# Graph attention with residual layer norm: three more output products put off to the end, unpaired norms after the last block, and the output bias of other late tiles added by VectorE

## The chip, the cores and the metric

The kernel runs on one core of one Trainium2 chip. The metric is device time in microseconds (us), the median of three runs. Engines are called PE (TensorE, matrix products), DVE (VectorE), ACT (ScalarE), POOL (GpSimd) and SP (SyncE, which here only issues DMAs). Line numbers such as L799 are those of the kernel before, as its profile shows them.

## The reference

One layer: multi-head attention over a graph, an output projection, a residual sum and a layer norm without scale or shift. x has 16 batches of 1024 rows of 512 numbers; there are 8 heads of 64. adj is a 1024 x 1024 matrix of zeros and ones, drawn with probabilities that fall with the row and column index, so most rows have few ones.

```python
q = (x @ Wq + bq).reshape(b, n, H, HD)
k = (x @ Wk + bk).reshape(b, n, H, HD)
v = (x @ Wv + bv).reshape(b, n, H, HD)
scores = jnp.einsum('bqhd,bkhd->bhqk', q, k) / jnp.sqrt(jnp.float32(HD))
scores = scores + (1.0 - adj)[None, None, :, :] * -1000000000.0
attn = jax.nn.softmax(scores, axis=-1)
out = jnp.einsum('bhqk,bkhd->bqhd', attn, v).reshape(b, n, d)
x = _layernorm(x + out @ Wo + bo)      # (y - mean) / sqrt(var + 1e-5)
```

## The kernel before

**Tiles.** The kernel sorts the rows of adj by their number of ones and works on 8 tiles of 128 rows per batch, rows of like degree together. A tile is named by batch and number, (b, t), and counted as 8 b + t. Batches from the third on are handled in pairs for the rows with the fewest neighbours; tile "mean" rows, tile 8 and tile 9 (`LONE_TILE`, `MORE_TILE`) collect such rows.

**Fronts.** For each batch PE transposes x and forms q, k and v (L757, L799 as `pq`, L956); the results go to DRAM. The list `fronts` holds these products as units with a cost, for all batches in order.

**Blocks.** Attention is done sparsely: one block is one neighbour of each of 128 rows. POOL gathers the neighbours' k and v by an indirect DMA (L1269), DVE multiplies and reduces (L1290, L1294), ACT takes the exponential (L1305) and weighs v (L1318) or DVE does (L1322), and DVE adds the block to the tile's sum (L1334). For tiles 6 and 7 a few deeper blocks are added on PE (`sum`, L1343 and L1344). When a tile closes, `normalise` divides by the denominator (L1355 to L1364), PE transposes the result (`poT`, L1378) and ACT copies it to `oT` (L1382).

**Output.** `finish(b, t)` then issues the output product of the tile, `po`, four units on PE (L799, each two records in the trace), and `complete` adds residual and bias on DVE with the row sum (L1108, L1109), squares on ACT (`spread`, L1116), scales the variance on DVE (L1119), takes the power -1/2 on POOL (L1122, or L1152 for two tiles at once), forms the shift on DVE (L1125), normalises on ACT (L1130) and stores rows by an indirect DMA from POOL (L1134). The output bias goes in one of three ways: as long as there are fronts (`plain`) DVE adds it in L1109; after that a small bf16 product on PE adds it within the output product (L1087); after the last block DVE adds it to the residual (L1076).

**Put-off tiles.** Tiles in `SPILL` don't get their output product in their own batch. Their `oT` is stored to DRAM by SP (L1384) and loaded again once the fronts are used up (`reload`, L1064), one every second step, into the buffers e, w and g in turn. Tiles in `STORED` have their residual rows saved in sorted order, and SP loads them from there (L1035); other residuals are gathered by POOL (L1038).

**Order.** All instructions are written out by hand in a loop over steps `n`, one per block (`tc.manual_schedule()`); each engine's queue has the order in which the loop issues its instructions. `later(k, fn)` puts a piece k steps on, `later_last` behind the other work of that step. In each step PE units are issued for as long as `credit` lasts, which grows by a share per step. In batches 1 to 12 that share is the PE work which the batch has to get done divided by its steps; `kept`, in that sum, counts the output products of tiles that aren't put off. From batch 13 on the share is set so that the fronts end 12 steps before the last batch, and after that it is 3.4 per step, where a unit of an output product counts 0.86. No product is begun in the last two steps before `total`, the step after the last block. After `total` the loop goes on until all products, stores and the guard (a test of number ranges that writes `flag`) are through.

**Pairs.** Once the fronts are over, norms are done for two tiles at a time: `half` keeps the first until the second comes, one power on POOL serves both. Tiles completed more than 3 steps after `total`, and shorter tiles, are done singly, with several steps between the stages.

Of the kernel before, what the change touches and what calls it, by code (L numbers as in the profile page):

```python
# [41 lines left out]

LAZY = 2

SPILL = (*(8 * b + t for b in range(4, 12) for t in (3, 6)), 102, 103, 106, 107)
STORED = {*SPILL, *(i for i in range(10, 102) if i % 8 in (2, 5, 7)), *(i for i in range(102, 128) if i % 8 > 1)}
LATE = 12

# [26 lines left out]
P = 128  # L75
# [103 lines left out]
def kernel(  # L179
# [75 lines left out]
    with ExitStack() as main:  # L255
# [85 lines left out]
        def tiles_of(b):  # L341
            return [t for t in range(NT) if t or b < PAIRED_FROM or merged(b)]

        def number(b, t):
            return b * NT + t if t < NT else -1
# [3 lines left out]
        x_rows = x.rearrange("b n d -> (b n) d")  # L349
        spill = {i: dram.tile([P, D], F32, name=f"spill_{i}") for i in SPILL}  # L350
        residual = {i: dram.tile([P, D], F32, name=f"residual_{i}") for i in sorted(STORED)}
# [94 lines left out]
        now, plan, rest, urgent, known, waiting, combined = [0], {}, {}, [], [], [], []  # L446

        def later(k, fn):
            plan.setdefault(now[0] + k, []).append(fn)

        def later_last(k, fn):
            rest.setdefault(now[0] + k, []).append(fn)
# [340 lines left out]
        def product(name, lhs, w, out):  # L793

            def unit(c):
                if c == 0:
                    PS[name] = fill_psum(name)
                p = PS[name]
                nc.tensor.matmul(p, lhs(c), w[:, c, :], start=(c == 0), stop=(c == NPAIR - 1))  # L799
                if c == NPAIR - 1:  # L800
                    del PS[name]
                    later(1, lambda: out(p))

            return [(PRODUCT, lambda c=c: unit(c), None) for c in range(NPAIR)]
# [210 lines left out]
        def rows_of(b, t):  # L1015

            if t == LONE_TILE or t == 0 and merged(b):
                n, col, base = (2 * SPARED, NT + 2, b - 1) if t else (P, NT + 1, b - 1)
            elif t == MORE_TILE:
                n, col, base = (LONE - SPARED) * (B - PAIRED_FROM), NT + 3, 0  # L1020
            else:
                n, col, base = P, NT if t == ONE_KEY and b >= PAIRED_FROM else t, b
            return n, asked_row[0:n, col:col + 1], base * N * D
# [30 lines left out]
        def keep_mean(b, p):  # L1054

            m = work.tile([1, D], F32, tag="q", name=f"out_mean_{b}", bufs=2)
            nc.scalar.copy(m, p[0:1, :])
            nc.sync.dma_start(mean_rows[b:b + 1, :], m)
            if merged(b):
                later(2, lambda: lone_tiles.append(b))  # L1060
# [7 lines left out]
        def finish(b, t):  # L1068


            mean_row = t == ONE_KEY and b >= PAIRED_FROM
            plain = bool(fronts) or mean_row
            biased = not plain and now[0] < total

            if now[0] >= total and not plain:
                nc.vector.tensor_tensor(Y[b, t], Y[b, t], bo_bc, op=OP.add)  # L1076

            def out(p):
                OT.pop((b, t))
                if mean_row:  # L1080
                    keep_mean(b, p)
                complete(b, t, p, plain)

            units = product(f"po_{b}_{t}", lambda c: OT[b, t][:, ts(c, P)], W["o"], out)
            if biased:
                def bias():
                    nc.tensor.matmul(  # L1087
                        PS[f"po_{b}_{t}"], three.to_broadcast([P, P]), bo_3, start=False, stop=False
                    )

                units.insert(2, (BIAS, bias, None))
            return units

        def complete(b, t, p, plain):
            n, rows, offset = rows_of(b, t)
            y, p = Y[b, t][0:n, :], p[0:n, :]
            single = fronts or now[0] > total + 3 or n < P
            if single:
                st = small.tile([P, 5], F32, name="stats", bufs=6)[0:n, :]
            else:  # L1100

                second = bool(half)
                if not second:
                    half.append([small.tile([P, 2, 5], F32, name="stats_2", bufs=5)])
                st2 = half[0][0]
                st = st2[:, int(second), :]
            if plain:
                nc.vector.tensor_tensor(y, p, y, op=OP.add)  # L1108
            nc.vector.scalar_tensor_tensor(  # L1109
                y, bo_bc[0:n, :] if plain else p, 1.0, y, op0=OP.mult, op1=OP.add, accum_out=st[:, 0:1]  # L1110
            )

            def spread():

                sq = work.tile([P, D], F32, tag="ysq", name=f"ysq_{b}_{t}", bufs=1)
                nc.scalar.activation(sq[0:n, :], y, AF.Square, bias=st[:, 0:1], scale=-float(D), accum_out=st[:, 2:3])  # L1116

            def variance():
                nc.vector.tensor_scalar(st[:, 2:3], st[:, 2:3], 1.0 / D ** 3, EPS, op0=OP.mult, op1=OP.add)  # L1119

            def power():
                nc.gpsimd.tensor_tensor(st[:, 3:4], st[:, 2:3], neg_half[0:n, :], op=OP.pow)  # L1122

            def shift():
                nc.vector.scalar_tensor_tensor(  # L1125
                    st[:, 4:5], st[:, 0:1], -1.0 / D, st[:, 3:4], op0=OP.mult, op1=OP.mult
                )

            def norm_out():
                nc.scalar.activation(y, y, AF.Identity, bias=st[:, 4:5], scale=st[:, 3:4])  # L1130
                later(2, store)

            def store():
                nc.gpsimd.indirect_dma_start(  # L1134
                    out=out_rows[b, t], out_offset=bass.IndirectOffsetOnAxis(ap=rows, axis=0),
                    in_=y, in_offset=None, element_offset=offset,
                )
                del Y[b, t]

            later_last(1, spread)  # L1140
            if single:
                late = 1 if fronts else 0
                later(2 + late, variance)
                later(3 + late, power)
                later(4 + 2 * late, shift)
                later_last(5 + 2 * late, norm_out)
            elif second:
                later(3, variance)
                mate_shift, mate_norm_out = half.pop()[1]

                def powers():
                    nc.gpsimd.tensor_tensor(  # L1152
                        st2[:, :, 3:4], st2[:, :, 2:3], neg_half[:, :, None].to_broadcast([P, 2, 1]), op=OP.pow
                    )

                def shifts():
                    mate_shift()
                    shift()

                later(4, powers)  # L1160
                later(6, shifts)
                later_last(6, mate_norm_out)
                later_last(7, norm_out)
            else:
                later(3, variance)
                mine = half[0]
                mine.append((shift, norm_out))

                def alone():
                    if half and half[0] is mine:  # L1170
                        half.pop()
                        power()
                        later(2, shift)
                        later_last(3, norm_out)

                later(6, alone)
# [197 lines left out]
        def turn(b, t, o):  # L1374
            def transpose():
# [4 lines left out]
                def out():  # L1380
                    OT[b, t] = work.tile([P, D], F32, tag="oT", name=f"oT_{b}_{t}", bufs=LAZY + 2)
                    nc.scalar.copy(OT[b, t], p)  # L1382
                    if number(b, t) in SPILL:
                        later(1, lambda: nc.sync.dma_start(spill[b * NT + t], OT.pop((b, t))))  # L1384
# [74 lines left out]
        done, coming, spilled, gathered, fronts, guarded = [], [], [], [0], [], []  # L1459

        total = len(blocks)

        def kept_y():
            return sum(t == "mean" or number(b, t) not in SPILL for b, t in Y)

# [25 lines left out]
        with tc.manual_schedule():  # L1491
# [9 lines left out]
            def needed(b, part):  # L1501
                b += int(part)
                if b >= B:
                    return fronts_time
                return fronts_by[b - 1] + (part - int(part)) * (fronts_by[b] - fronts_by[b - 1])
# [6 lines left out]
            n = -LEAD_IN  # L1512
            while n < total or plan or rest or urgent or done or finishing or spilled or lone_tiles or not guarded:
# [6 lines left out]
                elif n in start:  # L1520

                    b = start.index(n)
                    left = sum(u[0] for u in fronts)
                    ahead = EARLY + FIRST * (1 - max(0, b - 1) / LATE)
                    goal = fronts_time - needed(b + 2, ahead / NBT)
                    kept = sum(number(b, t) not in SPILL for t in tiles_of(b))
                    share = (max(0.0, left - goal) + kept * NPAIR * PRODUCT + NS * SUM) / (start[b + 1] - start[b])
# [105 lines left out]
```

## Time and profile before

| what | value |
|---|---|
| median of three runs | 1852.05 us (1851.02 to 1852.08) |
| profiled execution, its own time | 1859.34 us |
| its span, first to last instruction | 1857.6 us |
| PE busy (matmul) | 1807.5 us, 97% |
| DVE busy | 1686.4 us, 91% |
| ACT busy | 1565.1 us, 84% |
| POOL busy | 1247.5 us, 67% |
| mean granted clock of PE | 0.993 |
| output products `po` (L799), mean of one record | 600 ns (they overlap; eight of them follow each other in 3.43 us) |
| bias products (L1087) | 32 |

Busy time adds up what an engine's instructions took, and an idle engine may wait for data or for a buffer. The chain of waits follows the last instruction back through what released it each time. A timeline line gives the start, the length, the engine, the line, the operation and its tiles, and in brackets the idle time before it and what ended it.

### The profile page before, as it was taken

How to read it: one execution, taken by the hardware profiler on the slowest of the kernel's cores; microseconds unless marked ns; L12 is line 12 of the kernel's file. 1: busy time of each engine (PE TensorE's matmuls, PEld its weight loads, DVE VectorE, ACT ScalarE, POOL GpSimd, SP SyncE). 2: the span in 40 equal slices, each digit the busy share in tenths (PEclk: the TensorE clock that was granted, in tenths of full speed). 3: DMA queues.
4: the chain of work that ended last, by engine and by line, in shares of the span. 5: the costliest groups of instructions: out<-in, count | busy, mean ns of one | idle time of the engine just before them, and what ended most of it. 6: DMA issues, size and time to landing. Idle time of an engine off the chain costs nothing.

```text
span 1857.6 us, 25324 instructions
## 1 busy us (share of the span) xinstructions
PE 1807.5 (97%) x5150; PEld 878.6 (47%) x5150; DVE 1686.4 (91%) x3462; ACT 1565.1 (84%) x6184; POOL 1247.5 (67%) x1154
## 2 busy tenths in 40 slices
PE   7999999999999999999999999999999999999995
PEld 3444454544444444454444445454444444444442
DVE  6889889999989999999999999999999999997885
ACT  3637869989888898999789898989899999987885
POOL 1367866777666686667757676677767777665874
PEclk9999999999999999999999999999999999999998
DMA  7357797988888998999989998998989999888983
GB/s 285 111 187 244 245 324 250 335 305 315 301 299 295 312 323 303 330 312 310 316 312 310 331 321 299 342 319 314 346 285 331 318 352 318 311 313 317 361 305 120
DMA packets 195431, 553.82 MB, mean 298 GB/s; under 512 B 33162, under 2 KB 33182, under 8 KB 195266
## 3 DMA queue, kind: packets, MB, share of 16 engines
q0 software_dynamic: 113600, 373.64, 59.7%
q1 hardware_dynamic: 78590, 172.65, 24.9%
q10 hardware_dynamic: 3076, 5.82, 0.9%
q14 instruction: 122, 1.00, 0.2%
q8 instruction: 43, 0.70, 0.2%
HBM read 419.52 MB, written 153.51 MB: 308 GB/s over the span
## 4 chain that ended last, share of the span: by engine, by line
PE 69%; DVE 11%; ACT 8%; DMA 4%; issue 3%; POOL 1%; SPq 0%; POOLq 0%; DVEq 0%; ACTq 0%
PE po L799 17%; PE pq L799 14%; PE pp L956 12%; PE x L956 8%; PE z L956 8%; ACT pv L1318 5%; DVE qk L1290 2%; PE poT L1378 2%; PE pxT L757 2%; DMA kvg<-kv_pair,place_row 2%; DVE s L1294 2%; PE sum L1344 2%; PE sum L1343 2%; ACT sq_k L809 1%; DVE pv L1334 1%
## 5 line engine op out<-in xcount | busy, mean ns | idle before, releaser
L1318 ACT ACTIVATE pv<-kvg,pv 128x64 f32<-128x64 f32 x3600 | 907.3, 341 | 0.0
L1269 POOL DMA_INDIRECT kvg<-kv_pair,place_row x462 | 540.1, 1169 | 283.6 <-ACT pv L1318 89.5
L799 PE MATMUL po<-wo,oT 128*128 128x512 f32 x816 | 376.8, 600 | 0.4 <-ACT oT L1382 0.4
L799 PE MATMUL pq<-wq,xT 128*128 128x512 f32 x792 | 368.7, 597 | 1.9 <-DVE q L830 1.9
L1294 DVE TENSOR_REDUCE s<-qk 128x8 f32<-128x512 f32 x530 | 361.0, 681 | 6.7
L1290 DVE TENSOR_TENSOR qk<-qt,kvg 128x512 f32<-128x512 f32 x434 | 297.1, 685 | 3.1 <-DMA kvg<-kv_pair,place_row 2.9
L799 PEld LDWEIGHTS po<-wo,oT 128*128 128x128 f32 x816 | 155.3, 193 | 177.1 <-issue 167.9
L956 PE MATMUL x<-b,xT 128*128 128x512 f32 x504 | 237.1, 593 | 0.3 <-ACT e L969 0.2
L956 PE MATMUL pp<-t,s 128*128 128x512 f32 x504 | 237.0, 593 | 0.0
L1334 DVE TENSOR_TENSOR pv<-pv,pv 128x520 f32<-128x520 f32 x329 | 228.4, 694 | 3.8 <-ACT pv L1318 3.6
L799 PEld LDWEIGHTS pq<-wq,xT 128*128 128x128 f32 x792 | 148.4, 192 | 165.4 <-issue 152.6
L1010 POOL DMA_INDIRECT x<-in_x_dram,asked_row x120 | 132.3, 1103 | 75.0 <-PE pxT L757 22.1
L1134 POOL DMA_INDIRECT out_dram<-y,asked_row x129 | 146.9, 1139 | 40.4 <-issue 18.4
L1305 ACT ACTIVATE pv<-s,absent 128x8 f32<-128x8 f32 x434 | 126.9, 294 | 46.4 <-DVE s L1294 43.1
L809 ACT ACTIVATE sq_k<-kv 128x128 bf16<-128x128 f32 x512 | 150.8, 301 | 8.0 <-DVE kv L979 5.0
L956 PEld LDWEIGHTS pp<-t,s 128*128 128x128 f32 x504 | 94.3, 190 | 107.6 <-issue 98.4
L956 PEld LDWEIGHTS x<-b,xT 128*128 128x128 f32 x504 | 94.1, 190 | 106.2 <-issue 98.4
L1223 POOL DMA_INDIRECT qg<-q_rows,query_row x96 | 108.4, 1129 | 26.9 <-issue 24.5
L956 PE MATMUL z<-b,s 128*128 128x512 f32 x252 | 119.0, 595 | 3.7 <-DVE kv L984 3.7
L956 PE MATMUL z<-t,s 128*128 128x512 f32 x252 | 118.6, 593 | 0.0
L956 PE MATMUL pp<-t,xT 128*128 128x512 f32 x252 | 118.5, 593 | 0.0
L1130 ACT ACTIVATE y<-y,stats 128x512 f32<-128x512 f32 (+1 forms) x129 | 103.8, 807 | 17.2 <-DVE stats L1125 16.8
(276 smaller groups left out, 2710.4 us busy)
## 6 DMA issues: line engine op xcount, KB each, us to landing
kv_pair<-kv SPq DMA_DIRECT2D x98, 512.0 KB
q_rows<-q SPq DMA_DIRECT2D x106, 256.0 KB
qt<-q_rows SPq DMA_DIRECT2D x98, 256.0 KB
residual<-x SPq DMA_DIRECT2D x71, 256.0 KB
y<-residual SPq DMA_DIRECT2D x71, 256.0 KB
kv_rows<-kv SPq DMA_DIRECT2D x15, 512.0 KB
kvg<-kv_pair,place_row POOLq DMA_INDIRECT x462, 6.8
kv_pair<-kv SPq DMA_DIRECT2D x28, 256.0 KB
```

The lines of the kernel that those rows point to most:

```text
L799: nc.tensor.matmul(p, lhs(c), w[:, c, :], start=(c == 0), stop=(c == NPAIR - 1))
L809: nc.scalar.activation(sq, s[:, ts(h, P)], AF.Square, scale=scale, accum_out=sums[:, h:h + 1])
L956: nc.tensor.matmul(R[bank], l[:, ts(c, P)], right[:, c, :], start=(first and c == 0), stop=(c == 1), skip_group_check=True,)
L1010: nc.gpsimd.indirect_dma_start(out=y, out_offset=None, in_=x_rows, in_offset=bass.IndirectOffsetOnAxis(ap=asked_row[:, t:t + 1], axis=0), ...
L1134: nc.gpsimd.indirect_dma_start(out=out_rows[b, t], out_offset=bass.IndirectOffsetOnAxis(ap=rows, axis=0), in_=y, in_offset=None, element_o ...
L1223: nc.gpsimd.indirect_dma_start(out=q, out_offset=None, in_=q_rows[b % ROWS], in_offset=bass.IndirectOffsetOnAxis(ap=rows, axis=0))
L1269: nc.gpsimd.indirect_dma_start(out=KG[n], out_offset=None, in_=rows, in_offset=bass.IndirectOffsetOnAxis(ap=(place_row if b else key_row)[ ...
L1290: nc.vector.tensor_tensor(QK[n], q, KG[n][:, 0:D], op=OP.mult)
L1294: nc.vector.tensor_reduce(S[n], QK.pop(n).rearrange("p (h d) -> p h d", d=HD), axis=AX.X, op=OP.add)
L1305: nc.scalar.activation(PV[n][:, D:], S.pop(n), AF.Exp, bias=bias)
L1318: nc.scalar.activation(pv[:, ts(h, HD)], v[:, ds(D + h * HD, HD)], AF.Copy, scale=pv[:, D + h:D + h + 1])
L1334: nc.vector.tensor_tensor(PV[b, t], PV[b, t], pv, op=OP.add)
```

## The change

Three tiles join `SPILL`: 45, 69 and 93, that is tile 5 of batches 5, 8 and 11. After the fronts and before `total` only put-off tiles and tile 9 still get the bias as a product on PE; all others get it on DVE, added to the residual when the product begins. If a product ends in the last three steps before `total`, its `complete` is moved to `total`. Tiles completed from `total - 1` on are done singly, with one step from stage to stage, and their square in the step of the sum itself.

```diff
-SPILL = (*(8 * b + t for b in range(4, 12) for t in (3, 6)), 102, 103, 106, 107)
+SPILL = (*(8 * b + t for b in range(4, 12) for t in (3, 6)), 45, 69, 93, 102, 103, 106, 107)
...
-            biased = not plain and now[0] < total
-
-            if now[0] >= total and not plain:
+            biased = not plain and now[0] < total and number(b, t) in (*SPILL, -1)
+
+            if not plain and not biased:
                 nc.vector.tensor_tensor(Y[b, t], Y[b, t], bo_bc, op=OP.add)
 
             def out(p):
                 OT.pop((b, t))
                 if mean_row:
                     keep_mean(b, p)
-                complete(b, t, p, plain)
+                if not fronts and total - 4 < now[0] < total:
+                    later(total - now[0], lambda: complete(b, t, p, plain))
+                else:
+                    complete(b, t, p, plain)
...
-            single = fronts or now[0] > total + 3 or n < P
+            ending = not fronts and now[0] >= total - 1
+            single = fronts or ending or n < P
...
-            later_last(1, spread)
-            if single:
+            later_last(0 if ending else 1, spread)
+            if ending:
+                for step in (variance, power, shift):
+                    later(1, step)
+                later_last(1, norm_out)
+            elif single:
                 late = 1 if fronts else 0
                 later(2 + late, variance)
                 later(3 + late, power)
```

## The prediction

> **What bounds the kernel now.** I read the page first (PE 97%, DVE 91%, ACT 84% of a 1857.6 us span), then the busy times batch by batch, cut where the last reduction of a batch (L1372) stands. Shown are batches 5, 8, 10, 11 and 13; 5, 8 and 11 are those that lose a product.
>
> ```profile
> 702.18:804.59 102.41, 101.52 (x293) 49.69 (x293) 99.08 (x195) 93.36 (x388) 68.72 (x63) 1.00 0.92 321
> 1012.18:1112.54 100.36, 99.96 (x290) 49.17 (x289) 97.09 (x191) 90.62 (x368) 70.98 (x65) 1.00 0.93 320
> 1214.48:1313.24 98.76, 98.70 (x287) 48.58 (x286) 96.39 (x191) 92.23 (x371) 73.96 (x65) 1.00 0.92 327
> 1313.24:1419.84 106.60, 106.37 (x309) 52.13 (x308) 99.66 (x195) 96.14 (x397) 70.41 (x64) 1.00 0.88 311
> 1518.36:1614.15 95.79, 90.75 (x263) 44.32 (x262) 93.01 (x179) 89.56 (x377) 63.29 (x57) 0.98 0.92 323
> ```
>
> Columns: stretch, its length, busy us of PE, PE's weight loads, DVE, ACT, POOL, granted clock, DMA share, GB/s. TensorE lacks 0.2 to 0.9 us per batch, so these batches are as long as its work; VectorE stands just behind, up to 97.6% (batch 10), and in batch 13 (last line), where PE idles 5 us, DVE at 97.1% is what is left as a bound.
>
> Next the chain of waits, in order of time, for the end:
>
> ```profile
> 1785.81 0.22 PE po L1087
> 1786.03 3.43 PE po L799 x8
> ...
> 1828.96 1.19 PE sum L1343 x2
> 1830.16 0.88 PE sum L1344 x2
> 1831.04 3.42 PE po L799 x4
> 1834.45 0.42 PE po L1087
> 1834.88 1.83 PE po L799 x4
> 1836.77 0.58 issue
> 1837.43 0.62 DVE pv L1334
> ```
>
> One output product is eight records, 3.43 us; its bias product adds 0.22. Up to 1815.5 the chain is TensorE's products, then VectorE's, then the slow product of the last but one tile (5.7 us instead of 3.65). Last, the timeline of the tail:
>
> ```profile
> 1832.22 2.00 ACT L1318 ACTIVATE pv<-kvg,pv 128x64 f32<-128x64 f32 x8
> 1836.73 0.69 DVE L1109 SCALAR_TENSOR_TENSOR y<-po,y 128x512 f32<-128x512 f32 x1 [4.24 <-PE po L799]
> 1837.35 0.69 DVE L1334 TENSOR_TENSOR pv<-pv,pv 128x520 f32<-128x520 f32 x1
> 1848.67 0.58 POOL L1122 TENSOR_TENSOR stats<-stats,neg_half 128x1 f32<-128x1 f32 x1 [4.53 <-DVE stats L1119]
> 1849.45 1.04 POOL L1134 DMA_INDIRECT out_dram<-y,asked_row  x1 [0.20 <-issue]
> 1850.79 0.96 POOL L1134 DMA_INDIRECT out_dram<-y,asked_row  x1 [0.30 <-issue]
> ```
>
> The last attention sum (L1334) could start at 1834.2, when ACT's pv ends; it stands behind a y sum that waits 4.24 us for PE. After the last y sum: square, power on POOL, normalise, store; the store of 1850.79 is 6.8 us before the end of the span.
>
> **What the Trainium skill says.** "TensorE: Matmul & The Clock Gate" (Architectural detail) calls ACT and DVE strict FIFOs; the 4.24 us above agree. The same page (Part 1) halves the clock after about one idle window of 3.4 us; the trace shows clock 0.50 from 1830 to 1834 and from 1842 to 1844, after 2.78 and 3.04 us waits with little work around them. "Perfetto Trace Analysis" (Identifying the Most-Contended Engine) warns that matmul busy time is not distance to roofline; I use it only as queue time, since products follow each other every 3.43 us.
>
> **The change, part by part.**
>
> *Three products put off (tiles 45, 69, 93, batches 5, 8, 11).* Each batch loses 3.43 us of PE, and on DVE the two sums of L1108 and L1109 and two small steps: 0.61 + 0.69 + 0.15 + 0.15 = 1.6 us. ACT loses a square and a normalisation (0.9 + 0.8), POOL a power and a store. Added is one spill store on SP's queue (256 KB, 0.32 us to issue); a residual load and an output store of the same size go, so DMA moves 256 KB less of some 32 MB. These tiles are stored as residuals already. Is the 3.43 us got? PE alone says 3 x 3.43 = 10.3. If DVE can't go beyond the 97.6% of batch 10, batch 5 needs (99.08 - 1.6) / 0.976 = 99.9 us, which gains 2.5, batch 8 likewise 97.8, 2.5; batch 11 is still PE's, 3.4. I take 8.4. From below: DVE's own 1.6 each, 4.8; from above 10.3.
>
> *Fewer bias products.* The built order has 22 instead of 32. Up to the transpose of tile 7 of batch 15 as many products stand as before, with ten bias products fewer: 10 x 0.22 = 2.2 us of PE, on the chain up to 1815.5. Between 1720 and 1735 PE already waited 2.2 us for a spill load while DMA was full, so what the first three (po 3, 4, 5 of batch 14) save is likely to wait there: I take 1.5, ends 0 and 2.2. Instead DVE adds L1076, 0.61 us each, ten times before 1815.5. DVE was busy 133 of the 165 us from 1650 on, so these lie beside PE's products. The add stands earlier in the queue than the sum that needed the residual before, and waits for the load: for tile 4 of batch 15 SP issued it at 1787.4, landing takes 5.5 us in the median (2.7 to 7.8), and the add comes at about 1790.9, so 2 us are lost, with the next block's products behind it; DVE's waits for PE of 0.46, 0.58, 1.02, 1.44 and 1.14 us from 1795 to 1815 take that up. SP is not late: the load of po 7's residual waited to 1814.4, then come the last three spill loads, each behind the product that frees its buffer (1815.5, 1819.2, 1822.8); the first is needed at 1826.
>
> *The tail.* I follow the new queues in the times of before (all shifted alike by the two parts above). PE has a put-off product between the transpose of tile 7 and sum 6, then po 7, po 2, the transpose of 6, po 3, po 6. It fills the idle stretches, so the clock matters less; nothing below waits for it, even at half clock. DVE: the y sums of the two products that end near the last block are put behind the last attention sum, so that starts at 1834.2 instead of 1837.35 and o is ready at 1836.5: 3.1 us won. Then DVE does two reductions (0.24), two y sums and one add (1.85), two shifts (0.2): 1838.85. Now each tile has its own variance, power and shift: variance to power 0.24, power to shift 0.62, as at 1848.43, 1848.67, 1849.29, so 0.86 a rung and 0.15 for the shift. Two rungs: 1840.87. The y sum of po 2 (0.61), an add (0.61), the guard's five small steps (0.8): 1842.9, third power 1843.2 to 1843.8.
>
> In POOL's new order three powers stand before three stores, then power, three stores, power, store. A store takes 1.04 and 0.3 to the next. Stores from 1844.0 to 1847.65, fourth power to 1848.3 (its variance was ready at 1845.7: 2 us of queue), three stores to 1852.2, fifth power to 1852.85, shift 1852.9, normalise 1853.15 to 1853.95, store at 1854.2 (0.27 after an ACT end, as at 1831.88). Before: 1850.79. The tail costs 3.4 us, although its products themselves fit. Ends: +1 (powers that pass the stores sooner, because stores issue faster) and +5.5 (0.83 us powers, as at 1842.08, and a late third rung).
>
> *Sum.* -8.4 - 1.5 + 3.4 = -6.5 us. The profiled execution took 1859.34 (span 1857.6 and 1.74 around it), so 1852.8; it is 0.39% above the median of 1852.05, and the same share gives 1845.6.
>
> **Rivals.**
>
> *All of it gained.* PE is the only bound (10.3 + 2.2) and the tail comes out even: 1852.05 - 12.5 = 1839.5. For it: PE's missing 0.2 to 0.9 us per batch. Against: DVE at 96 to 98%, POOL's order.
>
> *The batches don't shorten beyond VectorE's share.* 4.8 gained, the bias saving lost to DMA, tail +3.4: 1850.6. For it: batch 13, and DMA at 0.92. Against: batches 4 to 11, with two tiles put off each, took 102.5 us on average, batches 2 and 3, with none, 105.3 and 112.8.
>
> *Slower: the adds wait for their residuals.* Ten adds stand before 1815.5. DVE's 32 us of idle there, less 6.1 for the adds and 2.2 that PE shortens, leave 24: from a mean wait of 2.4 us each on, DVE is the bound of the end. At 3.6 us the 12 us beyond come on top: about 1857.5. For it: the 2 us at tile 4. Against: most of SP's residual loads issue over 8 us ahead of use.
>
> **How the numbers follow.** Forecast 0.52, all gained 0.18, VectorE's share 0.20, adds late 0.10. What this measurement can't tell from no change is 0.2%, 3.7 us: 1848.35 to 1855.75. Faster: 0.48 of the forecast's 0.52 (its own range is 1841 to 1849.5), 0.18, and 0.05 of the third: 0.71. Same: 0.04 + 0.15 + 0.01 = 0.20. Slower: 0.09. Range 1838.5 to 1852: below it is the lower third of the second case, above it the late adds and the worst of the third.
>
> **What would show it.** Batches 5, 8 and 11 shorter by 2 to 3.4 us, the others as before; DVE at 98% there. 22 records of L1087's successor (L1090). L1076 fourteen times; a wait for a residual load before it at tile 4. The last pv sum right after ACT's pv, no 4.24 us wait. On POOL three stores between the third and fourth power and between the fourth and fifth, and the last store some 3 us later, counted from ACT's last pv. It is wrong if the batches keep their length, if PE waits for spill loads in the last 40 us, or if the last power isn't held up by stores.

## The result, and the profile after

The changed kernel takes 1850.74 us in the median of 12 runs (1847.92 to 1854.60), the kernel before, run beside it, 1854.72 us (1851.02 to 1859.03). The ratio is 0.9983, 95% interval 0.9975 to 0.9991: 0.17% faster, about 3.2 us (1.7 to 4.6 by the interval; the two medians lie 4.0 apart), where 0.35% was forecast. The forecast's 1845.6 us started from 1852.05, the median of three runs; the twelve runs beside the changed kernel put the kernel before at 1854.72. The profiled execution took 1851.61 us (span 1849.8), 7.7 us below the profiled one of before. That pair overstates the gain: the profiled execution of before was one of its longest. Batches 6 and 7 took 207.6 us in it, against 205.4 and 204.4 us in two other kernels that issue the same instructions in the same order there.

The page of the changed kernel, its span and the busy time of each engine:

```profile
span 1849.8 us, 25305 instructions
PE 1800.1 (97%) x5127; PEld 874.5 (47%) x5140; DVE 1691.9 (91%) x3472; ACT 1565.2 (85%) x6184; POOL 1249.1 (68%) x1154
```

The busy times of the changed kernel batch by batch, cut at the last reduction of a batch as before (batches 5, 8, 10, 11 and 13; the columns are those of the prediction: stretch, length, busy us of PE, weight loads, DVE, ACT, POOL, granted clock, DMA share, GB/s):

```profile
701.46:801.41 99.95, 99.57 (x286) 48.27 (x286) 97.73 (x190) 91.94 (x387) 69.18 (x62) 1.00 0.94 330
1005.91:1106.89 100.98, 98.03 (x281) 48.12 (x280) 95.96 (x187) 88.95 (x363) 68.24 (x65) 0.98 0.94 328
...
1209.24:1308.52 99.28, 99.24 (x288) 48.69 (x288) 96.38 (x191) 92.34 (x371) 75.59 (x66) 1.00 0.91 325
1308.52:1411.63 103.11, 102.31 (x300) 50.44 (x300) 98.20 (x191) 94.21 (x393) 67.28 (x62) 1.00 0.90 317
1509.57:1603.96 94.39, 89.69 (x263) 44.14 (x263) 92.89 (x179) 88.56 (x375) 62.88 (x57) 1.00 0.93 328
```

Batch 5 went from 102.41 to 99.95 us and batch 11 from 106.60 to 103.11. Batch 8, which lost a product as well, went from 100.36 to 100.98. It is the line to stop at: PE lacks 2.95 us of the stretch where it lacked 0.40 before, and its clock is 0.98.

The timeline of the tail, DVE and POOL around the last attention sum (start, length, engine, line, operation and tiles, idle time before it and what ended it):

```profile
1823.35 0.70 DVE L1342 TENSOR_TENSOR pv<-pv,pv 128x520 f32<-128x520 f32 x1 [1.75 <-ACT pv L1326]
...
1834.25 0.15 DVE L1123 TENSOR_SCALAR stats<-stats 128x1 f32<-128x1 f32 x1 [0.49 <-ACT ysq L1120]
...
1839.25 0.15 DVE L1123 TENSOR_SCALAR stats<-stats 128x1 f32<-128x1 f32 x1 [0.88 <-ACT ysq L1120]
...
1832.59 1.04 POOL L1138 DMA_INDIRECT out_dram<-y,asked_row  x1 [0.18 <-ACT y L1134]
1833.93 0.96 POOL L1138 DMA_INDIRECT out_dram<-y,asked_row  x1 [0.30 <-issue]
1835.20 0.96 POOL L1138 DMA_INDIRECT out_dram<-y,asked_row  x1 [0.30 <-issue]
1836.19 0.57 POOL L1126 TENSOR_TENSOR stats<-stats,neg_half 128x1 f32<-128x1 f32 x1
1836.95 1.53 POOL L1138 DMA_INDIRECT out_dram<-y,asked_row  x1 [0.19 <-issue]
...
1841.04 0.57 POOL L1126 TENSOR_TENSOR stats<-stats,neg_half 128x1 f32<-128x1 f32 x1
1842.99 1.04 POOL L1138 DMA_INDIRECT out_dram<-y,asked_row  x1 [1.38 <-ACT y L1134]
```

The last attention sum (L1342, which was L1334) now waits only for ACT's pv, which ends at 1823.31. The fourth and fifth powers (L1126) stand behind three stores each: their variances (L1123) were done at 1834.40 and 1839.40, they start at 1836.19 and 1841.04, 1.8 and 1.6 us later. From the end of ACT's last pv to the last store it is 19.7 us, before 16.6.

The chain of waits of the changed kernel (start, length, what held the end up) runs through the same places, from ACT's pv to the last sum and at the end through a store into the fifth power:

```profile
1821.41 1.92 ACT pv L1326 x8
...
1823.35 0.71 DVE pv L1342
...
1840.05 0.96 POOL out_dram L1138
...
1841.04 0.57 POOL stats L1126
```

### The profile page after: what moved, and what is told of

Same layout as the page of the kernel before. It is cut to its first block, busy times and chain, and to the rows that moved or that the text cites. A ratio compares the mean times of both kernels' runs of the same rounds, so it can differ in the third digit from the quotient of the medians.

```text
span 1849.8 us, 25305 instructions
## 1 busy us (share of the span) xinstructions
PE 1800.1 (97%) x5127; PEld 874.5 (47%) x5140; DVE 1691.9 (91%) x3472; ACT 1565.2 (85%) x6184; POOL 1249.1 (68%) x1154
## 4 chain that ended last, share of the span: by engine, by line
PE 72%; DVE 11%; DMA 5%; ACT 4%; issue 3%; POOL 1%; SPq 0%; POOLq 0%; DVEq 0%; ACTq 0%
PE po L799 17%; PE pq L799 15%; PE pp L956 13%; PE z L956 9%; PE x L956 9%; ACT pv L1326 2%; PE pxT L757 2%; DVE qk L1298 2%; PE poT L1386 2%; DVE s L1302 2%; PE sum L1352 2%; PE sum L1351 2%; DMA kvg<-kv_pair,place_row 2%; DVE pv L1342 1%; DMA oTs<-spill 1%
## 5 line engine op out<-in xcount | busy, mean ns | idle before, releaser
L1277 POOL DMA_INDIRECT kvg<-kv_pair,place_row x462 | 532.2, 1152 | 289.0 <-ACT pv L1326 89.8
L799 PE MATMUL po<-wo,oT 128*128 128x512 f32 x792 | 359.2, 593 | 0.2 <-ACT oT L1390 0.2
L1342 DVE TENSOR_TENSOR pv<-pv,pv 128x520 f32<-128x520 f32 x329 | 228.3, 694 | 4.4 <-ACT pv L1326 4.2
L799 PEld LDWEIGHTS po<-wo,oT 128*128 128x128 f32 x792 | 148.6, 190 | 169.5 <-issue 160.6
L1010 POOL DMA_INDIRECT x<-in_x_dram,asked_row x120 | 136.2, 1135 | 65.8 <-issue 21.2
```

The lines of the kernel that those rows point to most:

```text
L1010: nc.gpsimd.indirect_dma_start(out=y, out_offset=None, in_=x_rows, in_offset=bass.IndirectOffsetOnAxis(ap=asked_row[:, t:t + 1], axis=0), ...
L1277: nc.gpsimd.indirect_dma_start(out=KG[n], out_offset=None, in_=rows, in_offset=bass.IndirectOffsetOnAxis(ap=(place_row if b else key_row)[ ...
L1342: nc.vector.tensor_tensor(PV[b, t], PV[b, t], pv, op=OP.add)
```

## The experiments

Ratios are against the kernel before on the same chip. The first four runs fell on a chip whose times are those of above. The others fell on chips where every kernel takes 0.9 to 1.7% longer, most of it in batch 0 (286 to 297 us instead of 277), and where runs of one kernel differ by 10 us and more. There the lengths of batches in the traces tell more than totals, though they scatter too.

*The three products taken out for good.* All three are stored and never fetched again, so their rows of the output are not written:

```
 SPILL = (*(8 * b + t for b in range(4, 12) for t in (3, 6)), 45, 69, 93, 102, 103, 106, 107)
+NEVER = 45, 69, 93
...
-                        spilled.append((b, t))
+                        if number(b, t) not in NEVER:
+                            spilled.append((b, t))
```

> The kernel before, with the attention outputs of tile 5 of batches 5, 8 and 11 stored to DRAM and never fetched again: their output product, layer norm and store of rows are left out for good, so those 384 rows are not written. It measures what the three products cost inside their batches, with nothing given back at the end. My sum says 8.4 us less than before (2.8 a tile; if TensorE's share alone decided, 10.3). The rival that only VectorE's share comes back says 4.8 us less (1.6 a tile). The theory that the rest of the batch takes up the gap (another engine's work becomes the bound there) says under 3 us. If it is 8 or more, the front term of my sum was right and the bias term or the end is what failed.

Measured: 1848.31 us, ratio 0.9963 (0.9947 to 0.9979): 6.9 us less, interval 3.9 to 9.8. The size of the sum is possible, 4.8 is too.

*Only the list of put-off products* (the SPILL line alone).

> The kernel before with only the list of put-off products made longer by three; the bias of the last tiles stays on TensorE and the end keeps its paired norms. The three products move to the last batches, where TensorE has more to do. My sum says that nothing is won by moving work alone unless the last two batches have room for it: the front gives -8.4 us and the end takes three products (10.3 us of TensorE) less the gaps they fill there. In after, batches 14 and 15 were 3.7 us shorter with all parts together. I expect -2 to -5 us against before; the theory that the products find no gap at the end says 0 to +2.

Measured: 1851.36 us, ratio 0.9982 (0.9973 to 0.9991), 3.3 us less: as expected, and as much as the whole change.

*Only the bias.*

```
-            biased = not plain and now[0] < total
+            biased = not plain and now[0] < total and number(b, t) in (*SPILL, -1)
...
-            if now[0] >= total and not plain:
+            if not plain and not biased:
```

> The kernel before with only the bias of the last tiles that were not put off moved from TensorE to VectorE's sum with the residual. My sum says -1.5 us (bounds 0 and -2.2). The rival theory, that TensorE then only reaches its wait for a fetched attention output sooner and loses the time there, says -0.5 to 0. That the sums wait for residuals and hold up VectorE says above 0.

Measured: 1852.42 us, ratio 0.9987 (0.9979 to 0.9995), 2.4 us less (0.9 to 3.9). Alone it brings what I gave it, or more.

*Only the end* (completions put off, norms unpaired; 20 tiles put off as before).

> The kernel before with only the end changed: the last completions are put off until the attention is done, and the norms there are unpaired. Removing the wait at the last attention sum should give 3.1 us there, and the stores in GpSimd's queue between the powers should take some of it back: from ACT's last pv to the end of the span 23.4 us before, 26.5 us in after. Theory: the span from ACT's last pv grows by 2 to 3.5 us, the batch before it shrinks by about 3, so the whole is -1 to +1 us. If the tail change is a pure loss, +2 to +3.5 us.

Measured: 1854.34 us, ratio 0.9999 (0.9991 to 1.0008): nothing, as expected of the total. The way there was not the expected one. The stretch behind ACT's last pv, expected to grow by 2 to 3.5 us, grew by 0.3 (23.69 us, before 23.38).

These four already show where the lack is. Kernels that issue the same instructions in the same order in a batch need nearly the same time for it (the chance of it is seen within each group of three). Lengths in us, from six traces of the same speed:

| batch | before | bias_only | tail_only | after | drop3 | spill_only | with three less |
|---|---|---|---|---|---|---|---|
| 5 | 102.41 | 102.41 | 102.60 | 99.95 | 100.03 | 99.95 | -2.5 |
| 8 | 100.36 | 100.42 | 100.37 | 100.98 | 100.99 | 100.76 | +0.5 |
| 9 | 101.94 | 101.89 | 101.93 | 102.35 | 102.35 | 102.34 | +0.4 |
| 11 | 106.60 | 106.25 | 106.65 | 103.11 | 103.11 | 103.75 | -3.2 |
| 12, 13 | 194.31 | 193.52 | 193.99 | 192.33 | 192.32 | 193.26 | -1.3 |

(12 and 13 are the sum of two; the last column is the mean of the last three kernels less that of the first three.) From the start of batch 5 to the end of 13 it is 908.8 us in the mean of bias_only and tail_only and 902.7 in the mean of the three with the products gone: 6.1 us, where the sum had 8.4. (The trace of the kernel before, 912.0 us, is left out of that mean for its long batches 6 and 7.) Batch 8 gives nothing. Its timeline in the changed kernel, PE first and then DVE:

```profile
1061.42 1.88 PE L956 MATMUL z<-t,s 128*128 128x512 f32 x4
1063.14 1.88 PE L956 MATMUL pp<-t,xT 128*128 128x512 f32 x4
1067.97 3.67 PE L956 MATMUL z<-b,s 128*128 128x512 f32 x4 [2.95 <-DVE kv L984]
...
1065.76 0.42 DVE L783 TENSOR_TENSOR s<-xT 128x256 f32<-128x256 f32 x1 [0.29 <-ACT xT L761]
...
1067.23 0.68 DVE L984 TENSOR_TENSOR kv<-z,g 128x512 f32<-128x512 f32 x1
```

and in the kernel before:

```profile
1067.72 1.88 PE L956 MATMUL z<-t,s 128*128 128x512 f32 x4
...
1071.16 0.60 PE L1378 MATMUL poT<-ident,o 128*128 128x128 f32 x4
1071.59 1.88 PE L956 MATMUL z<-b,s 128*128 128x512 f32 x4
...
1069.64 0.69 DVE L984 TENSOR_TENSOR kv<-z,g 128x512 f32<-128x512 f32 x1 [0.94 <-PE z L956]
```

The two z products of a pair add into one PSUM tile, and VectorE's L984 must read it between them. Before, the plan put the first z product two blocks ahead of the second; L984 (waiting 0.94 us for it) ran as soon as it was done, and the second z found it read. With a product less the plan puts the first z into the block just ahead of the second, L984 into VectorE's next block, behind a score reduction and four sums of 256 columns, and PE stands 2.95 us for it. The product behind the wait runs at half clock (3.67 us for four records instead of 1.88). So PE loses about 4.7 us (2.95 and the 1.79 that the product took longer) where it had been spared 3.43.

On the other chips, in the runs below, the same order repeats less well. Batch 5 took 102.2 us instead of 100.0 in after_again and spill_tail_b, about half of that from work that had moved there out of a shorter batch 4. In spill_tail_b batch 8 took 104.23 us, with longer waits (4.15 us at L984) whose cause I don't know.

*Two products instead of three, and another batch instead of batch 8* (in the changed kernel `45, 93` and `45, 77, 93` in place of `45, 69, 93`).

> The changed kernel with two products put off instead of three: tile 5 of batch 8 is left where it was. In all three traces with that product gone, batch 8 took 0.5 us more than in the three with it (100.91 against 100.38), because TensorE waits 2.95 us for L984's successor once and then runs one product at half clock. Theory that the product of batch 8 brings nothing: batch 8 back at 100.4, batch 9 at 101.9 instead of 102.35, the end shorter by part of a product, 0 to 1 us for the rest, so the whole is 0 to 2.5 us below the changed kernel. Rival: the loss in batch 8 is made good later (in batches 9 to 13, which were 1.4 us shorter together), so it is 1 to 2 us above the changed kernel. My first sum, 2.5 us for this product, says 2.5 us above it.

> The changed kernel with tile 5 of batch 9 put off in place of tile 5 of batch 8. In batch 9 TensorE is busy 101.9 of 101.9 us and VectorE 96.7, so by the shares of my first sum it should lose all 3.4 us, with batch 8 back at 100.4: together 3.5 to 4 us below the changed kernel, batch 9 at 98.5. Rival: what a batch gives back is set by where the new plan puts the neighbours of the missing product and not by the shares, so batch 9 may lose anything from 0 to 3.4 us: -0.5 to -4 us. If the whole is above the changed kernel, both are wrong.

Measured: after_two 1879.55 us, ratio 0.9972 (0.9950 to 0.9994); after_77 1875.67 us, ratio 0.9935 (0.9919 to 0.9952), without the changed kernel beside them. In the traces batch 8 did not come back at 100.4 but took 106.48 and 106.42 us (with all three put off, spill_bias and spill_tail took 99.87 and 100.93 us on the same chip), then batch 9 101.14 and 99.62. Batches 8 to 10 of after_two, by busy times:

```profile
1026.47:1132.95 106.48, 104.40 (x298) 50.38 (x296) 97.16 (x192) 94.33 (x378) 72.40 (x68) 1.00 0.91 315
1132.95:1234.09 101.14, 98.96 (x290) 48.82 (x292) 96.61 (x190) 91.60 (x377) 65.57 (x61) 1.00 0.89 309
1234.09:1336.14 102.05, 99.28 (x286) 48.04 (x285) 96.39 (x190) 92.87 (x371) 72.08 (x65) 1.00 0.90 316
```

PE has as many products as before there (874 records; before 877) and lacks 7.0 us instead of 0.5: a product missing in batch 5 and none in batch 8 makes the plan of batch 8 worse than either of the other lists does. Both my theories on these two fell, and they share their ground: I priced a batch by its shares, or took over the old batch 8, while each list gives a new order. For after_77 the total (11 us less than before, only 6 runs) and its trace (batches 5 to 13 in 910.1 us, the changed kernel 902.5, 908.4 and 903.5 in three traces) don't agree; I leave it open.

*The bias and the end in company*: spill_tail is the changed kernel with the bias on TensorE, spill_bias the one with the old end.

> The changed kernel with the bias of the last tiles back on TensorE (32 bias products instead of 22, no sums of the bias with the residual before the end). Alone, moving the bias brought 2.4 us (interval 0.9 to 3.9). If the saving adds up, this is 1.5 to 2.4 us above the changed kernel. If in company it is lost to the wait for the fetched attention output near 1720 (0.7 us alone, 1.9 us and four records at half clock in the changed kernel), it is within 0.5 us of the changed kernel.

> The changed kernel with the end as before: completions not put off, norms in pairs. Its stores then don't stand between as many powers, but the last attention sum waits again for two products. By my sum the changed end wins 3.1 us at the last attention sum and loses it again behind it, so this is within 1 us of the changed kernel, with the stretch from ACT's last pv to the end longer by about 1 us or shorter by as much. If the changed end is worth its 3 us, it is 2 to 3 us above; if it is a loss, 1 to 3 us below.

Measured: 0.9971 (0.9954 to 0.9987) and 0.9954 (0.9939 to 0.9969), without the changed kernel beside them, so only their traces answer. From ACT's last pv to the end of the span spill_bias takes 26.85 us, the changed kernel 26.49: the new end is worth nothing there, with three more tiles too. With the bias on TensorE it costs 1.1 us there (spill_only, with the old end, 25.39; spill_tail_c 26.48).

*The order of one pair.* The changed kernel, with the first z product of the pair that is prepared in batch 8 issued before the transposes instead of behind them:

```
-            units += xt
-            units += unit("z", s(1), T1, True, out_v1, None)
+            z = unit("z", s(1), T1, True, out_v1, None)
+            units += z + xt if (b, j) == (10, 0) else xt + z
```

> The changed kernel once more, for a second trace and as the measure for the other three runs on this chip. From its first runs: 0.17% below the kernel before (interval 0.09 to 0.25). Batch 8 again with a wait of 2.95 us of TensorE for VectorE's L984, since that comes from the order of the instructions and not from this one execution.

> The changed kernel with one pair's order changed (tiles 0 and 1 of batch 10, which are prepared in batch 8): the first z product stands before the transposes of the next tiles instead of behind them, so VectorE's sum that empties it comes one block earlier and the second z product finds it done. The same instructions, 28 of TensorE's rows moved. Theory: the wait of 2.95 us and the half clock behind it go, batch 8 takes about 98.3 us (VectorE's 95.96 us at its 97.6%), the whole is 2.5 to 3 us below the changed kernel, and the product put off in batch 8 is then worth what my first sum gave it. Rival: TensorE only meets VectorE a few products later, batch 8 and 9 keep 203.3 us together, no change.

> The changed kernel with the bias of the last tiles back on TensorE, again, now beside the changed kernel on the same chip. If the bias saving adds up in company it is 1.5 to 2.4 us above the changed kernel; if it is lost to the wait for a fetched attention output or to VectorE behind TensorE at the last but one transpose (4.49 us of wait when moved alone, 2.75 before), within 0.7 us.

> The z product placed as in z_first, with three products put off and the bias on VectorE, but the end as in the kernel before (norms in pairs, completions not put off). If the changed end is worth nothing, as it was alone (0.2 us), this equals z_first within 1 us. If the stores between the powers cost more with three more tiles at the end, it is 1 to 3 us below z_first, and the best of all.

Measured: 0.9961 (0.9930 to 0.9993) for the changed kernel, 0.9954 (0.9928 to 0.9981), 0.9980 (0.9950 to 1.0010) and 0.9947 (0.9921 to 0.9974), six runs each: too wide to part them. The wait of L984 is gone in z_first and z_first_pairs and stands at 2.96 us in the changed kernel. Batches 8 and 9 took 200.60 us in z_first but 203.38 in z_first_pairs, where PE waited 1.82 us for a q sum of VectorE and then ran a product at half clock; the changed kernel beside them (after_again) took 201.65. So three of these kernels ran again:

> The changed kernel once more, as the measure for the next two runs on the same chip and as a third trace of batch 8: TensorE waits 2.95 us for L984 there, batches 8 and 9 take 201.7 to 203.3 us together (203.33 and 201.65 so far, with and without half clock behind the wait).

> The kernel of z_first again, on this chip. So far it stood in one trace at 200.60 us for batches 8 and 9 and in another of the same order at 203.38, with the wait of L984 gone in both, but 1.0 and 1.8 us of wait for VectorE's q sum 13 us later. If the order of that one pair is what ate the product of batch 8, this is 2.5 to 3 us below the changed kernel and the two batches take 200.3 us. If VectorE holds TensorE up a little later instead, the two batches take at least 202 us and the whole is within 1 us of the changed kernel.

> The changed kernel with the bias of the last tiles back on TensorE, beside the changed kernel on the same chip. If the bias saving adds up in company it is 1.5 to 2.4 us above the changed kernel, with batches 14 and 15 together 1.5 to 2.2 us longer; if it is lost to waits, within 0.7 us.

Measured, 20 runs each: the changed kernel 1866.97 us, ratio 0.9970 (0.9951 to 0.9989); z_first_b 1862.14 us, 0.9955 (0.9938 to 0.9972); spill_tail_c 1867.50 us, 0.9986 (0.9971 to 1.0001). Mean against mean, z_first_b is 3.7 us below the changed kernel (+-2.8, from the scatter of the 20 runs). Busy times of batches 8 and 9, the changed kernel (after_c):

```profile
1021.47:1122.46 100.99, 98.04 (x281) 48.07 (x280) 95.91 (x187) 88.96 (x363) 69.87 (x65) 0.98 0.92 324
1122.46:1224.80 102.34, 102.34 (x301) 50.41 (x300) 96.66 (x190) 94.14 (x389) 67.63 (x62) 1.00 0.90 311
```

and z_first_b:

```profile
1016.37:1115.41 99.04, 99.04 (x288) 48.78 (x287) 95.36 (x187) 90.64 (x369) 69.95 (x65) 1.00 0.95 334
1115.41:1216.23 100.82, 99.33 (x293) 49.01 (x292) 96.66 (x190) 92.39 (x382) 66.16 (x61) 1.00 0.88 310
```

The pair's two z products in z_first_b, from PE's timeline, with no wait before the second:

```profile
1070.30 1.88 PE L956 MATMUL z<-t,s 128*128 128x512 f32 x4
...
1075.04 1.88 PE L956 MATMUL z<-b,s 128*128 128x512 f32 x4
```

PE lacks nothing in batch 8 any more, and the two batches take 199.86 us instead of 203.33: 3.5 us less, and 2.4 less than in tail_only, which has the product in it (202.30). In this trace, with the wait gone, the product is worth the 2.5 us of my sum; in z_first it is worth 1.7, in z_first_pairs nothing (203.38). A wait of 1.49 us for VectorE's q sum is left in batch 9; it is what came to 1.82 us in z_first_pairs. By the totals of 20 runs this order beats both kernels.

## Why the prediction was wrong

The ends of the last batches, from the close of batch 13, in us:

| kernel | put off | bias on | end | to the end of ACT's last pv | from there to the end |
|---|---|---|---|---|---|
| before | 20 | PE | old | 220.07 | 23.38 |
| tail_only | 20 | PE | new | 217.75 | 23.69 |
| drop3 | 20 | PE | old | 218.37 | 23.19 |
| bias_only | 20 | DVE | old | 218.31 | 21.89 |
| spill_only | 23 | PE | old | 220.07 | 25.39 |
| spill_tail | 23 | PE | new | 221.37 | 26.46 |
| spill_tail_b | 23 | PE | new | 221.48 | 26.49 |
| spill_tail_c | 23 | PE | new | 219.96 | 26.48 |
| spill_bias | 23 | DVE | old | 218.87 | 26.85 |
| z_first_pairs | 23 | DVE | old | 219.34 | 26.76 |
| after | 23 | DVE | new | 219.35 | 26.49 |
| after_again | 23 | DVE | new | 221.41 | 26.56 |
| after_c | 23 | DVE | new | 219.73 | 26.57 |
| z_first | 23 | DVE | new | 222.29 | 26.52 |
| z_first_b | 23 | DVE | new | 219.80 | 26.54 |

*The three products, -8.4 in the sum: 6.1 measured, and this is the step that failed.* "If DVE can't go beyond the 97.6% of batch 10 ... batch 8 likewise 97.8, 2.5." The sum took it that a batch shortens to what the shares of its busiest engines allow. Batches 5 and 11 did: 2.5 us and 3.2 less (forecast 2.5 and 3.4). Batch 8 took 0.5 us more and batch 9, forecast as before, 0.4 more. The share of a batch says how much room there is and not whether the new order uses it: VectorE stood at 95.0% in batch 8. What took the gain was one wait, PE's for L984, which stood late in VectorE's queue, and a half clock behind it.

Moving that one product shows it: the wait is gone in all three traces with z_first's order, and the whole is 3.7 us shorter (+-2.8) on the one chip with 20 runs. The traces also part the wait from the half clock. Batches 8 and 9 took 203.1 to 203.5 us with both (six traces), 201.65 and 201.98 with the wait and no half clock (after_again, spill_bias), and 199.86 and 200.60 with neither. So, as an estimate from these few traces, the wait costs 1 to 2 us and the half clock about 1.5. In z_first_pairs the loss came back at the next meeting of the two engines.

The Trainium skill, "TensorE: Matmul & The Clock Gate" (Architectural detail), says that VectorE takes its instructions strictly in order; here that made a sum whose input had been ready since about 1063.3 start at 1067.23.

Part of the 6.1 is chance as well. Of the 1.3 us less in batches 12 and 13, most is a half clock in batch 13: before, bias_only and tail_only each had one there, behind a wait of 2.0 to 2.7 us (95.3 to 95.8 us), and so had spill_only (95.35), while after and drop3 had waits of 2.68 and 2.67 us without one (94.39). With it, as in spill_only, batches 5 to 13 gained 5.4 us.

*The bias, -1.5 in the sum: not settled in company.* The ten products are gone, as forecast. With 23 tiles put off the stretch to ACT's last pv is 220.0 to 221.5 us with the bias on PE (four traces, mean 220.7) and 218.9 to 222.3 with it on DVE (seven, mean 220.1): 0.6 us less in the mean, within a scatter of more than 3. By total times the bias in company is worth 1.7 us +-2.7 (spill_tail_c against after_c). Neither tells the forecast's 1.5 us from nothing. In the changed kernel's own trace PE loses time at two places: where the prediction said that it might, at the wait for a fetched output, and at the transpose of tile 7. From PE's timeline:

```profile
1722.65 3.13 PE L799 MATMUL po<-wo,oTs 128*128 128x512 f32 x4 [1.89 <-DMA oTs<-spill]
1814.63 0.65 PE L1386 MATMUL poT<-ident,o 128*128 128x128 f32 x4 [3.11 <-DVE o L1372]
```

The same two places in the kernel before:

```profile
1734.32 1.99 PE L799 MATMUL po<-wo,oTs 128*128 128x512 f32 x4 [2.20 <-DMA oTs<-spill]
1825.53 0.66 PE L1378 MATMUL poT<-ident,o 128*128 128x128 f32 x4 [2.75 <-DVE o L1364]
```

The first wait is not longer, 1.89 us for 2.20, but the four records behind it ran at half clock, 3.13 us instead of 1.99. In the other traces this wait was between nothing and 2.9 us, so it is chance in good part. The second wait is 3.11 us for 2.75.

Alone the bias brought 2.4 us, and not ahead of ACT's last pv: bias_only reaches that after 218.31 us, two of the three kernels with 20 tiles and the bias on PE after 217.75 and 218.37. PE waits longer there at the transpose of tile 7:

```profile
1819.33 0.66 PE L1378 MATMUL poT<-ident,o 128*128 128x128 f32 x4 [4.49 <-DVE stats L1119]
```

bias_only is shorter behind the last pv (21.89 against 23.2 to 23.7). With 23 tiles put off and the new end the place of the bias makes no difference there (26.46 to 26.49 on PE, 26.49 to 26.57 on DVE).

*The tail, +3.4 in the sum: 3.1 measured, in part for another reason.* Order and waits came as worked out: three powers, three stores, power, three stores, power, store; the last sum 3.1 us earlier behind ACT's pv. The held-up powers cost 1.8 and 1.6 us. But the new end with 20 tiles (tail_only) needs only 23.69 us behind the last pv, and the old end with 23 (spill_bias) 26.85. It is the three more tiles that cost there, in either order: 2.0 us from before to spill_only, 2.8 from tail_only to spill_tail_c, 5.0 from bias_only to spill_bias, pairs that differ in nothing else. Behind the last pv stand ten stores instead of seven in all of them. That the size came out so near is partly luck, since the sum laid it to the order of stores and powers, and the old order costs as much.

*Sum.* -6.1 + 3.1 = -3.0 us, with the bias of the traces (0.6) -3.6, beside 3.2 measured (1.7 to 4.6). One item isn't in it: up to ACT's last pv the kernels with the bias on PE took 218.7 us in the mean with 20 tiles put off and 220.7 with 23. With these 2.0 us the sum is -1.6. That lies within what the stretch scatters, and I can't tell it from nothing.

*The signs to look for.* L1090 stands there 22 times by its weight loads (16 records of the products themselves are in the trace), L1076 14 times: as forecast. The wait for a residual load before L1076 is 0.5 us in all, not 2. The landing time behind those 2 us, 5.5 us (2.7 to 7.8), was misread: it is that of the DMAs that POOL issues on y, and the trace has none for SP's loads. VectorE at 98% holds in batch 5 (97.8), not in 8 (95.0) and 11 (95.2, where PE is the bound as worked out). PE waits for no fetched output in the last 40 us.

*The rivals.* "Not beyond VectorE's share" forecast 1850.6 us, next to the 1850.74 measured, but that is luck: it is 1.4 us below a start of 1852.05, and the measured gain is 3.2. Its front term (1.6 us a tile) is wrong, batches 5 and 11 gave 2.5 and 3.2. "All gained" fell with batch 8. The adds don't wait for residuals: VectorE's late arrival in bias_only, where PE's wait at one transpose grew by 1.74 us, is what is left of that fear.

## What to carry to other kernels

When a planner places work by credits, as this one does, taking work out of a stretch gives a new order. Price it by the shares, and then look, in the order that is built, for the places where two instructions that meet over one buffer have moved from two blocks apart to one. Here it was one such place.

To find a gain of a few us that total times hardly show, compare the lengths of stretches between kernels whose order is the same there. In the six traces of the first chip, batches 5, 8, 9 and 11 of one order repeated within 0.7 us, most within 0.2, where totals scatter by 4 us and more. One trace is not enough even so: on the other chips batch 5 of one order differed by 2.3 us and batch 8 by 4.4.

## What was not expected of the hardware

An idle TensorE of 2.94 to 2.98 us at one and the same place in batch 8 (eight traces) was followed by half clock six times and twice not: the four records behind it took 2.86 to 3.67 us in the six and 1.98 and 1.99 in the two. In batch 13 a wait of 2.67 us ended with half clock in spill_only (95.35 us) and without it in drop3 (94.39), and at 1722.65 in the changed kernel one of 1.89 us ended with it. The Trainium skill, "TensorE: Matmul & The Clock Gate" (Part 1), lets the clock fall after about one idle window of 3.4 us. The waits here are shorter, so as a safe length of a wait that figure does not hold in this kernel. The page also says that the window runs freely and isn't set back when a kernel starts; if so, the same wait can fall into it differently each time, but no run here shows the window. The half clock made batch 8 about 1 us longer (100.98 against 99.84 in after_again).
